# A two-layer graph and expert network on one core: mask casts issued late as transfers, the input in five loads, powers in pairs, and a written-out issue order

## The chip, the cores and the metric

The kernel runs on one core of a Trainium2 chip. The metric is the device time of one execution in microseconds (us). A core has five engines with in-order queues of their own: TensorE (PE, matmuls; PEld, its weight loads), VectorE (DVE), ScalarE (ACT), GpSimd (POOL) and SyncE (SP, which here only issues transfers). Sixteen DMA engines serve the transfers that SyncE, ScalarE and GpSimd issue.

## The reference, cut to what matters

There are 2708 rows of 256 features and a dense 2708 x 2708 matrix `adj` whose non-zero entries are large (up to 1e9, about 1% of all). Each of two layers adds a graph attention and then a block with eight experts to the rows:

```python
# layer 0
x = x + _L0_gnn_ref(_layernorm(x, axis=-1), adj, ...)      # softmax(leaky_relu(..) + adj) @ h
x = x + _L0_ffn_ref((_layernorm(x, axis=-1))[None], ...)   # causal attention, then top-2 of 8 experts
# layer 1
x = x + _L1_gnn_ref(_layernorm(x, axis=-1), adj, ...)      # mask = (adj != 0) | eye; softmax; sigmoid(attn @ Xp)
x = x + _L1_ffn_ref((_layernorm(x, axis=-1))[None], ...)   # top-2 of 8 experts
return x
```

In layer 0 `adj` is added to the logits, so with entries that large each row's softmax picks the row's largest entry: the graph attention is a gather of one projected row. In layer 1 only `adj != 0` matters. The kernel tests on the chip that these readings hold for its input and has a general path behind a flag, which is not run here.

## The kernel before, in words

Rows are worked on in 22 tiles of 128 (the last has 20). There are four stages: `first` (layer 0 up to the router and three early expert blocks), `experts_blocks` of layer 0, `second` (layer 1's graph attention and router), `experts_blocks` of layer 1.

`first` and `second` don't issue their instructions in program order. Each adds steps to a `Plan` (L75): a step has an engine, an assumed length, a function that issues its instructions, the steps that it needs, named buffers that it takes and gives, a rank, and `lands`, the time by which a transfer's data comes after its issue. `issue` (L125) walks an assumed clock: it finds the steps that can start soonest, and among those of one engine that can start within `NEAR` of that it issues the one of lowest rank. That fixes the order in every engine's queue; the chip then runs these queues in order, with waits on semaphores. When TensorE would idle in the plan for `GAP_MIN` or more, `fill` puts filler matmuls (`nobody`, L1288 and L1691: a constant tile against itself) into the gap, `FILL` of it at `UNIT` each.

The first stage, by its steps:

- Loads on SyncE: `x` in three transfers (four tiles, 17 tiles, the last; L856, L859), then weights (L868, L870).
- `project(t0)` for a pair of tiles, eleven in all: `stats` (VectorE mean and variance, L268, L270, L918), `power` (GpSimd, the reciprocal root, one per tile, L922), `turn` (transposes, L929), `bias` (GpSimd, L933), `back` (ScalarE, L938), `times` (matmuls with the centred weight, L949), `out_` (ScalarE scales, L956), `store` (to the DRAM tensor `hd`, issued by ScalarE, L961).
- `tile_in(t)` for a tile: `load` of a row block of `adj` (1354 KB, one of three ring buffers `adj0..2` in `arena`, L990) and of the rope table (L992); `top` (L995) and `index` (L999), VectorE's search for the largest entry and its place; `narrow` (L1009), ScalarE's cast of the block to bf16 in two halves, with GpSimd memsets of the padding (L1006, L1008); `save` (L1012), which stores the halves in the DRAM tensor `mb` for the second stage; `fetch` (L1017), GpSimd's gather of the chosen rows of `hd`, added to the tile; then statistics (VectorE), `power` (GpSimd, L1029, L1030), `norm` and `leave` (ScalarE), transposes and `times` (TensorE, L1038, L1047), the rope in `both` (GpSimd, L804 to L806, L1064) and `turn_qk`, `keep` (L1070, L1073). A ring buffer is taken by `adj` and `low` names: it is free again when both `index` and the second `narrow` have read it. The first `narrow` also waits for the last projected rows in DRAM.
- `pair(t0)`: causal attention of two tiles against all tiles before them. Per earlier tile `scores` (L1121), `exps` (ScalarE, L1127), `mask` on the diagonal (GpSimd, L1136), `values` (L1147), and `sums` (VectorE, L1161, L1166; the first three pairs sum on TensorE). Then `spread`, `turn_over` (VectorE's reciprocal, L1204), `weigh` (GpSimd, L1208), `project_out` (L1222), `join` (L1226), `sum_up` (GpSimd, L1229), `store` (L1232).
- `route` after the pairs at 4, 10, 16, 18 and 20: the router's logits, choice, places, and `send` (L1830), GpSimd's scatters of rows to the experts' lists `xs`.
- At the end three early expert blocks (L562, L585), whose weights go into `arena` when the ring is free, and whose results GpSimd adds to DRAM (L622).

The experts' stage (L2115, L2130) starts with a transfer of rows of `xs` and so after all scatters. `second` reads `mb` with transposing transfers as its masks.

`before` is a constant strict triangle, made by a GpSimd iota and a VectorE comparison (L232); `allones` is set by GpSimd alone (L229).

Of the kernel before, what the change touches and what calls it, by code (L numbers as in the profile page):

```python
# [20 lines left out]
P = 128  # L21
N = 2708
# [51 lines left out]

class Plan:  # L75
# [8 lines left out]
    UNIT = 0.24  # L84
    FILL = 0.75
    GAP_MIN = 1.0
# [38 lines left out]
    def issue(self, behind=0.0):  # L125
# [25 lines left out]
def adj_ffn_kernel(ctx, tc, x, adj, vecs, bias_rows, tab, w_gnn0, w_gnn1, wqkv, wo,  # L151
# [41 lines left out]

    ident = const.tile([P, P], F32, name="ident")
# [33 lines left out]
    allones = const.tile([P, P], F32, name="allones")  # L228
    nc.gpsimd.memset(allones, 1.0)  # L229

# [138 lines left out]

    def route(add, tiles, ready, copied, cleared, layer, XB, xs, pool, turn_tile, turn_bank, gate_tile, gate_bank, rank):  # L370
# [127 lines left out]
        if layer == 0:  # L498
            a = [add("ACT", 0.6, lambda t=t: squares(t), [ready[t - t0]], rank=rank) for t in tiles]
            a = add("DVE", 0.3, mean, a, rank=rank)  # L500
            scaled = add("POOL", 0.9, power, [a], rank=rank)
        last = None
        for pair in pairs:
# [10 lines left out]
            if gate_tile is None:  # L514
                a = add("ACT", 0.25, lambda pair=pair: keep(pair), [a], give=[turn_bank], rank=rank)
            last = a
        a = add("DVE", 3.2, choose, [last], rank=rank)
        b = add("ACT", 0.5, exps, [a], rank=rank)
# [3 lines left out]
        return [add("POOL", 2.7, lambda t=t: send(t), [b, c] + cleared, rank=rank + 6, lands=2.0) for t in tiles]  # L522


    def some_blocks(add, layer, blocks, fetched, needs, weights, xs, acc, new, named, rank):

        joins = []
        for k, (e, j, before) in enumerate(blocks):
# [68 lines left out]
            a = add("ACT", 0.7, back, [a], take=[names["xT"]], give=[names["mm"]], rank=r)  # L597
# [3 lines left out]
            a = add("ACT", 1.4, gate, [a], take=[names["sl"], names["hT"]], rank=r)  # L601
            a = add("DVE", 1.4, times, [a], give=names["up"] + [names["sl"]], rank=r)
# [4 lines left out]
            joins.append(add("POOL", 1.6, join, [a], give=[names["ys"]], rank=r))  # L607
        return joins

    def early_blocks(add, layer, needs, sent, *rest):  # L610
        blocks = [(e, j, (needs if layer == 0 else []) + sum([sent[t] for t in sent if t < before_t], []))
                  for e, j, before_t in EARLY[layer]]
# [196 lines left out]
    def first(X, XB, norms, tops, hd, mb, xs, acc, arena, load_weights):  # L809
# [11 lines left out]
        with ExitStack() as s:  # L821
# [24 lines left out]
            def tr_tile():  # L846
                return mm_tile().rearrange("p (k c) -> p k c", c=P)

            plan = Plan(mm=2, mv=4, ix=4, tb=6, st=2, o=1, zs=1, e=4, xg=3, hT=3,
                        z=2, qk=2, es=1, ob=2, yT=2, mb=2, rT=1, adj0=1, adj1=1, adj2=1, low0=1, low1=1, low2=1)  # L850
# [396 lines left out]
            for t in range(NT):  # L1247
                tile_in(t)
# [1194 lines left out]
```

## Time and profile before

| what | us |
|---|---|
| median of 3 runs | 1467.53 (1466.63 to 1470.84) |
| the profiled execution | 1465.13 |
| its span, first to last instruction | 1463.3 |
| PE busy in the span | 1385.9 (95%) |
| DVE, ACT, POOL busy | 775.9, 555.3, 525.3 |
| mask casts on ACT (L1009), 44 | 57.2, 1323 ns each |
| gathers' issues on POOL (L1017), 22 | 37.2, 1691 ns each |
| filler matmuls of `first` (L1288), 220 | 33.4 |

The profile is of one execution. Busy time is by engine; a matmul's end is modelled, so a busy TensorE isn't one at its peak. "Chain of waits" is the chain of work that ended last, followed back from the last instruction. "Releaser" is what ended an engine's idle time. The granted clock is the share of TensorE's full clock that the throttle let through. Lines like L1009 are lines of the kernel printed above.

### The profile page before, as it was taken

The numbers are of one execution on the slowest core, as the hardware profiler recorded it, in microseconds if no ns is written. First come the engines' busy times: TensorE is split into PE (matmuls) and PEld (weight loads), VectorE is DVE, ScalarE is ACT, GpSimd is POOL, SyncE is SP. The second block draws the span as 40 slices with busy tenths as digits, with TensorE's granted clock in tenths as the row PEclk, the third lists the DMA queues.
The fourth block names the chain that finished last, engine by engine and source line by source line (L and its number), as shares of the span: only waits on it lengthen the run. The fifth ranks groups of instructions, "written<-read, shape, count | busy, mean of one in ns | idle before, by whom it ended". The sixth has DMA issues, their size and how long they took to land.

```text
span 1463.3 us, 20902 instructions
## 1 busy us (share of the span) xinstructions
PE 1385.9 (95%) x7218; PEld 1006.3 (69%) x7218; DVE 775.9 (53%) x1680; ACT 555.3 (38%) x1104; POOL 525.3 (36%) x677
## 2 busy tenths in 40 slices
PE   6988989989999999999999899999999999999996
PEld 5643433433343888888788878888768888878885
DVE  5688999985676432222222474768565322322221
ACT  2576867655545322222221444434432211111110
POOL 5576668874224312222222210022334222222222
PEclk9899999999999999999999999999999999999998
DMA  7588756540001277777512770616321687666211
GB/s 268 192 290 287 252 197 226 158 155 31 8 16 64 46 205 185 168 175 197 105 18 26 159 166 1 133 39 151 108 73 58 148 214 187 194 185 129 24 19 21
DMA packets 260056, 193.05 MB, mean 132 GB/s; under 512 B 168008, under 2 KB 232104, under 8 KB 257232
## 3 DMA queue, kind: packets, MB, share of 16 engines
q1 hardware_dynamic: 235638, 162.32, 38.0%
q0 software_dynamic: 20032, 25.71, 9.7%
q10 hardware_dynamic: 4270, 3.58, 0.8%
q8 instruction: 59, 0.97, 0.3%
q14 instruction: 57, 0.47, 0.1%
HBM read 119.81 MB, written 56.11 MB: 120 GB/s over the span
## 4 chain that ended last, share of the span: by engine, by line
PE 77%; DVE 8%; POOL 6%; DMA 5%; issue 2%; ACT 1%; SPq 0%; POOLq 0%; DVEq 0%; ACTq 0%
PE pup L2115 23%; PE po L1603 15%; PE y L2130 13%; PE o L1147 4%; PE stt L1121 4%; PE up L562 3%; DMA X<-hd,ix 3%; PE pup L2146 3%; PE y L2180 1%; DVE yT L1204 1%; DVE es L1166 1%; PE po L949 1%; DVE ix L999 1%; POOL ra L804 1%; DVE tops L995 1%
## 5 line engine op out<-in xcount | busy, mean ns | idle before, releaser
L2115 PE MATMUL pup<-xTs,arena 128*128 128x256 f32 (+2 forms) x1320 | 249.7, 348 | 0.6 <-ACT xTs L2098 0.6
L2115 PEld LDWEIGHTS pup<-xTs,arena 128*128 128x128 f32 (+1 forms) x1320 | 218.5, 189 | 27.2 <-PE y L2180 1.5
L1603 PE MATMUL po<-hb,PT 128*128 128x257 f32 (+2 forms) x968 | 227.6, 389 | 2.9 <-DVE PT L1596 2.9
L2119 ACT ACTIVATE sl<-pup 128x256 f32<-128x256 f32 (+1 forms) x210 | 73.5, 350 | 368.9 <-PE pup L2115 325.4
L1603 PEld LDWEIGHTS po<-hb,PT 128*128 128x128 f32 (+2 forms) x968 | 176.7, 189 | 42.8 <-issue 13.3
L2120 DVE TENSOR_TENSOR hT<-sl,pup 128x256 f32<-128x256 f32 (+1 forms) x210 | 79.6, 380 | 225.8 <-ACT sl L2119 220.5
L1127 ACT ACTIVATE e<-stt 128x1024 f32<-128x1024 f32 (+1 forms) x132 | 125.5, 986 | 93.5 <-PE stt L1121 63.8
L1166 DVE TENSOR_TENSOR es<-es,e 128x1024 f32<-128x1024 f32 x104 | 137.8, 1325 | 29.8 <-ACT e L1127 22.0
L622 POOL DMA_INDIRECT out<-ys,XR x44 | 68.0, 1545 | 234.2 <-DVE ys L2133 149.5
L622 POOL DMA_INDIRECT acc<-ys,XR x44 | 68.3, 1553 | 215.4 <-DVE ys L2133 120.8
L1121 PE MATMUL stt<-qT,kT 64*128 64x512 f32 (+1 forms) x528 | 133.4, 616 | 4.3 <-ACT e L1127 3.9
L2130 PE MATMUL y<-arena,hT 128*128 128x256 f32 x612 | 137.3, 380 | 0.0
L2130 PEld LDWEIGHTS y<-arena,hT 128*128 128x128 f32 x612 | 114.6, 190 | 19.7 <-DVE hid L2154 4.9
L1830 POOL DMA_INDIRECT xs<-XR,place x88 | 93.2, 1059 | 91.8 <-DVE mk L1590 40.2
L1147 PE MATMUL o<-e,V 128*64 128x512 f32 (+1 forms) x528 | 122.4, 586 | 0.0
L1581 ACT ACTIVATE E<-sb,dcol 128x768 f32<-128x768 f32 (+1 forms) x88 | 75.3, 859 | 108.4 <-DVE PT L1596 106.5
L2133 DVE TENSOR_SCALAR ys<-y,XR 128x256 f32<-128x256 f32 x71 | 34.4, 484 | 133.7 <-PE y L2130 133.7
L2115 PE MATMUL pup<-xTs,room 128*128 128x256 f32 (+3 forms) x528 | 99.9, 346 | 0.0
L1121 PEld LDWEIGHTS stt<-qT,kT 64*128 64x128 f32 x528 | 44.7, 188 | 76.5 <-issue 63.0
L2115 PEld LDWEIGHTS pup<-xTs,room 128*128 128x128 f32 (+1 forms) x528 | 85.4, 189 | 9.8 <-PE y L2180 0.8
L1147 PEld LDWEIGHTS o<-e,V 128*64 128x64 f32 x528 | 32.9, 136 | 68.5 <-issue 53.2
L995 DVE MAX8 tops<-arena 128x8 f32<-128x2708 f32 (+1 forms) x22 | 65.3, 2970 | 1.5 <-DMA arena<-in_adj 1.5
(319 smaller groups left out, 1972.1 us busy)
## 6 DMA issues: line engine op xcount, KB each, us to landing
more<-in_w SPq DMA_DIRECT2D x48, 640.0 KB
arena<-in_adj SPq DMA_DIRECT2D x21, 1354.0 KB
arena<-in_w SPq DMA_DIRECT2D x36, 640.0 KB
mb<-mb SPq DMA_DIRECT2D x44, 352.0 KB
xs<-none SPq DMA_DIRECT2D x16, 536.0 KB
room<-in_w SPq DMA_DIRECT2D x12, 640.0 KB
pieces<-xs SPq DMA_DIRECT2D x200, 32.0 KB
acc<-X SPq DMA_DIRECT2D x21, 128.0 KB
```

What stands on the lines that cost most here:

```text
L622: i = nc.gpsimd.indirect_dma_start(out=acc[:, :], out_offset=bass.IndirectOffsetOnAxis(ap=tokens.bitcast(I32), axis=0), in_=ys, in_offset= ...
L995: nc.vector.max(out=tops[:r, t, :], in_=v["a"][:r])
L1121: nc.tensor.matmul(st[:r, g, c0(sb):], kT[a:b, sb * P:sb * P + r], qT[a:b, t0 + (sb == t0 + 1):t0 + 2, :, :], start=True, stop=True)
L1127: nc.scalar.activation(e[:r, :, c0(sb):], v[sb, "st"][:r, :, c0(sb):], AF.Exp, scale=1.0 / HD ** 0.5)
L1147: nc.tensor.matmul(v["o"][g * HD:(g + 1) * HD, c:], V[:r, sb, g * HD:(g + 1) * HD], v[sb][:r, g, c:], start=(n + i == 0), stop=(n + i == t ...
L1166: nc.vector.tensor_tensor(es, es, v[sb][:r, :, c:], ALU.add)
L1581: nc.scalar.activation(e[:q, :n], sb[:q, i0:i1], AF.Exp, bias=dcol[:q, j:j + 1], scale=SLOPE - 1.0)
L1603: nc.tensor.matmul(v["po", i][:r, :F], v["PT", j][:q, a:a + r], hb[:q, j, :], start=(j == 0), stop=(j == NT - 1))
L1830: i = nc.gpsimd.indirect_dma_start(out=xs[:, :], out_offset=bass.IndirectOffsetOnAxis(ap=at, axis=0), in_=src, in_offset=None)
L2115: nc.tensor.matmul(pp[:to, i, :B, :], wn[:, c, :], xT[:, c, :B, :], start=(c == 0), stop=(c == KC - 1))
L2120: nc.vector.tensor_tensor(hT[:, n, :B, :], sl[:, :B, :], pp[:, 1, :B, :], ALU.mult)
L2130: nc.tensor.matmul(y, hT[:, n, b, :], w[3][:, n, :], start=(n == 0), stop=(n == NHC - 1))
```

## The change

What it does, part by part:

- The mask casts leave `tile_in`. `narrow`, its memsets and `save` go, and the buffers `low0..2` and `mb` with them. In their place stand 22 steps `cast` on GpSimd, each a transfer that reads a row block of `adj` from DRAM a second time and writes it to `mb` as bf16. They need the load of the last tile and, in the plan, one another. A step `blank` on SyncE writes zeros to the padding of `mb`.
- `x` comes in five loads (tiles 0-1, 2-5, 6-13, 14-20, 21). The rope table has a step of its own.
- `project` takes the statistics of two tiles into one buffer and makes one scaling and one `power` for the pair.
- The index results of all tiles have room of their own (`ixs`), not four buffers in turn.
- `allones` is set earlier, and the fillers multiply `allones` by itself. `UNIT` becomes 0.22, `FILL` 0.85, `GAP_MIN` 0.7.
- `issue` takes a list that gives every step its rank: `ORDERS[0]` with 1233 numbers for `first`, `ORDERS[1]` with 1128 for `second`. In the first list the tiles' searches stand as 0, 1, 3, 2, 4, 6, 10, 5, 7, 8, 9, 11, 12, 13, 14, 16, 15, 17, 19, 20, 21, 18; the casts stand between the fourth pair's `weigh` and the last pair's `mask`, the last five gathers among them.
- Assumed lengths and `lands` are changed throughout, and some needs are added that order steps (an expert's `join` after the stores of its rows; one router's choice after the one before; two empty steps at the end of each stage).

```diff
-    UNIT = 0.24
-    FILL = 0.75
-    GAP_MIN = 1.0
+    UNIT = 0.22
+    FILL = 0.85
+    GAP_MIN = 0.7
...
-    def issue(self, behind=0.0):
+    def issue(self, order, behind=0.0):
+        assert len(order) == len(self.steps), len(self.steps)
+        for step, n in zip(self.steps, order):
+            step["rank"] = n
...
-            plan = Plan(mm=2, mv=4, ix=4, tb=6, st=2, o=1, zs=1, e=4, xg=3, hT=3,
-                        z=2, qk=2, es=1, ob=2, yT=2, mb=2, rT=1, adj0=1, adj1=1, adj2=1, low0=1, low1=1, low2=1)
+            plan = Plan(mm=2, mv=4, mvp=4, tb=6, st=2, o=1, zs=1, e=4, xg=3, hT=3,
+                        z=2, qk=2, es=1, ob=2, yT=2, rT=1, adj0=1, adj1=1, adj2=1)
...
-            for a, b in ((0, 4), (4, NT - 1)):
-                loads.append(add("SP", 0.5, lambda a=a, b=b: nc.sync.dma_start(
+            loads, ends = [], (2, 6, 14, NT - 1)
+            for a, b in zip((0,) + ends, ends):
+                loads.append(add("SP", 0.55 * (b - a), lambda a=a, b=b: nc.sync.dma_start(
...
+                def power():
+                    for at, q in [((0, 2), P)] if rows(t0 + 1) == P else [((0, 1), P), ((1, 2), rows(t0 + 1))]:
+                        n = at[1] - at[0]
+                        nc.gpsimd.tensor_tensor(out=rsx[:q, t0 + at[0]:t0 + at[1]], in0=v["pv"][:q, at[0]:at[1], 0],
+                                                in1=mhalf[:q, :n], op=ALU.pow)
...
-                    nc.scalar.copy(m[:r, :b - a], v["a"][:r, a:b])
-
-                def save(h):
-                    nc.sync.dma_start(out=mb[t * P:(t + 1) * P, h * HALF:(h + 1) * HALF], in_=v["m", h])
+                def cast():
+                    nc.gpsimd.dma_start(out=mb[t * P:t * P + r, :N], in_=adj[t * P:t * P + r, :])
...
-                a = loaded[t] = add("SP", 5.8, load, take=[f"adj{t % 3}", f"low{t % 3}", "tb"], rank=rank,
-                                    lands=1.5)
-                a = add("DVE", 2.97, top, [a], rank=rank + 2)
-                b = a
-                for h in range(2):
-
-                    b = add("ACT", 1.4, lambda h=h: narrow(h), [b, stored[-1]], take=["mb"], give=[f"low{t % 3}"] * h, rank=rank + 4)
-                    add("SP", 0.4, lambda h=h: save(h), [b], give=["mb"], rank=rank, lands=3.0)
-                a = add("DVE", 3.05, index, [a], take=["ix"], give=[f"adj{t % 3}"], rank=rank + 2)
+                a = loaded[t] = add("SP", 3.6, load, take=[f"adj{t % 3}"], rank=rank - 2.0, lands=2.0)
+                tb = add("SP", 0.4, load_tb, take=["tb"], rank=rank, lands=2.2)
+                a = add("DVE", 3.0, top, [a], rank=rank)
+                a = add("DVE", 2.97, index, [a], give=[f"adj{t % 3}"], rank=rank)
...
+            add("SP", 3.0, blank, [loaded[NT - 1]], rank=NT + 4.0, lands=3.0)
+            last = None
+            for t, cast in enumerate(casts):
+                last = add("POOL", 1.2, cast, [loaded[NT - 1], last], rank=NT + 0.5 * t, lands=6.0)
...
-                        nc.tensor.matmul(nobody[:, :P], allones, before, start=True, stop=True)
+                        nc.tensor.matmul(nobody[:, :P], allones, allones, start=True, stop=True)
...
-                plan.issue()
+                plan.issue(ORDERS[0])
```

## The prediction

> **What bounds the kernel now.** I read the busy time by stretches first, then the same stretches for the filler matmuls alone, then the chain of waits, then SyncE's queue and the DMA queues. The stretches follow the work: projections (to 60 us), attention limited by VectorE (to 260), attention limited by TensorE (to 480), the tail (to 510), the experts of layer 0 (to 800), the second stage (to 1150), the experts of layer 1. Columns: stretch, length, then busy us of PE, PEld, DVE, ACT and POOL, the granted clock, the DMA share and GB/s.
>
> ```profile
> 0.00:60.00 60.00, 44.37 (x224) 38.17 (x225) 37.48 (x101) 22.01 (x46) 35.12 (x74) 0.89 0.65 213
> 60.00:260.00 200.00, 175.62 (x786) 77.40 (x784) 182.10 (x179) 143.81 (x256) 146.64 (x204) 0.97 0.77 255
> 260.00:480.00 220.00, 209.00 (x958) 82.97 (x957) 160.47 (x205) 121.19 (x192) 107.28 (x135) 1.00 0.21 66
> 480.00:510.00 30.00, 27.55 (x194) 24.71 (x193) 10.79 (x45) 10.12 (x25) 12.79 (x17) 1.00 0.25 51
> 510.00:800.00 290.00, 290.00 (x1622) 245.42 (x1622) 85.83 (x243) 68.55 (x190) 64.09 (x48) 1.00 0.56 136
> 800.00:1150.00 350.00, 339.49 (x1799) 284.51 (x1798) 210.39 (x647) 137.76 (x253) 90.60 (x153) 0.99 0.41 98
> ```
>
> From 510 to 800 us TensorE has no gap, and in the second stage it lacks 10.5 of 350 us. Only the first stage has room. Its fillers are no work, so they come off (the tile `nobody` alone, PE and PEld):
>
> ```profile
> 0.00:60.00 60.00, 11.36 (x60) 10.96 (x61) 0.89 0.65 213
> 60.00:260.00 200.00, 15.38 (x112) 13.97 (x110) 0.97 0.77 255
> ```
>
> TensorE's real work is 44.4 - 11.4 = 33 us of the first 60, 175.6 - 15.4 = 160 of the next 200 (a rate of 0.80), 209.0 - 3.3 = 206 of 220, 27.6 - 3.5 = 24 of 30: 423 us in 510, so 87 us are not work. VectorE is the other bound: 182 of 200 us from 60 to 260, mostly the 44 searches of 2.97 us (L995, L999), which the change keeps. The chain of waits (start, length, what) says what holds both up early:
>
> ```profile
> 9.29 4.10 PE nobody L1288 x22
> 19.44 10.29 DMA hd<-hs
> 57.04 9.35 DMA X<-hd,ix
> 83.15 7.37 DMA X<-hd,ix
> 112.17 10.10 DMA X<-hd,ix
> 166.52 8.48 DMA X<-hd,ix
> 283.30 4.65 DMA X<-hd,ix
> ```
>
> The gather of a tile takes 7.4 to 10.1 us while the DMA engines are 0.77 busy, and 4.65 us when they are quiet. The fillers are the first link on TensorE: they wait for a tile (`before`, L232) that VectorE makes only after four row statistics, and the first transposes (13.2 us) stand behind them although their rows landed at 5.6. In SyncE's queue the reader is to see that nothing is issued between the third mask row load and the first mask save:
>
> ```profile
> 17.92 0.35 SPq L990 DMA_DIRECT2D arena<-in_adj  x1
> ...
> 54.86 1.55 SPq L1012 DMA_DIRECT2D mb<-mb  x2
> 56.51 0.94 SPq L990 DMA_DIRECT2D arena<-in_adj  x1
> ```
>
> The fourth load (56.5 us) is queued behind a save whose ScalarE cast waits for the last projected rows; its buffer was read by the first index search at 38.6.
>
> **The change part by part.** Sums are against the profiled execution: 1465.13 us, of which 1463.3 are the span; it lies 2.4 us under the median of the three runs (1467.53).
>
> *Fillers from `allones` on both sides.* That tile is set by GpSimd at 2.4 us. The fillers can run from there, and the first real transposes start when two row tiles (256 KB instead of 512 KB) have landed, 4 to 6 us instead of 13.2. Gain at the head between 0 (if the projections are then held by the store of 10.29 us or by VectorE's 22 statistics, 22 x 0.76 = 17 us) and 9. More filler (0.85 of a gap from 0.7 us on) costs at most one filler run before a real step, some 1 us each for a few dozen runs, from 0 to 10 in all. I take 8 off for the head and 0 for the runs, since they are sized to gaps.
>
> *X in five loads.* The same 2.7 MB; four more issues on SyncE by 0.48 us, beside the landing of the first. Nothing.
>
> *Powers in pairs.* 11 of 22 powers of 0.55 us go (6 us of POOL) and 10 scalings of 0.15 on VectorE. Off the chain; each pair's first power now waits for the second tile's statistics, 0.76 us, hidden behind the matmuls of 1.9. Nothing.
>
> *The casts leave ScalarE.* 44 casts of 1.32 us = 57 us go from ScalarE before 295 us, 47 of them before 240, and with them 44 saves (15.5 MB) from SyncE and the DMA engines, and 10.7 us of memsets from POOL. SyncE no longer blocks at 18 to 55 us, and a mask row buffer comes free at the index search. What is late next is VectorE itself: it was idle 60 - 37.5 = 22.5 us before 60 and 17.9 from there to 260, some 40 us, of which about 6 at the start can't be filled. 40 of the saves, 14 MB of some 64 moved (213 GB/s for 60 us, 255 for 200), fall before 260, so the DMA share drops by about a fifth. Four gathers on the chain at 4.65 instead of 35.3 in all is 16.7 us at best, 0 at worst (the loads may run ahead and fill the engines again).
>
> *The casts come back as 22 transfers from DRAM to DRAM, issued by POOL.* The issue: no row shows one. Nearest are the gathers' issues, 1.46 to 2.44 us, median 1.64: 22 x 1.64 = 36 us of POOL. The list puts the first one behind the fourth pair's weighting (L1208, 184 us in this trace) and the last one before the masks of the last pair, so nearly all lies in a stretch where POOL has 220 - 107 = 113 us free. Behind each on POOL are masks, scatters and the rope of late tiles; a delay of 1.6 us there is covered by e's four buffers. Without that cover it would be the 36 us.
>
> The Trainium skill, "SBUF — State Buffer", in its warning on DVE blocking DMA, speaks against this: descriptors of a DMA issued by GpSimd can't be written while VectorE holds the shared port, and 620 ns became 3100. By that the casts would take 22 x 3.1 = 68 us of POOL, an estimate that still fits into those 113; the gathers' issues here rose to 2.44 at most beside a VectorE 91% busy.
>
> Their transfers: POOL's queue q0 took 9.7% of 16 engines' span for 25.71 MB, which is 88 engine-us per MB; SyncE's q1 took 38.0% for 162.32 MB, 55. A tile of 1.39 MB read is thus 4.8 us (q1's rate) to 7.7 (q0's), and 11.5 if the 0.69 MB written count too. I take 7.7, q0's, since it is the same queue: 22 x 7.7 = 169 us beside a DMA share of 0.21. It costs nothing on the path if it is over when the last scatters need the same queue (near 480 us).
>
> The DRAM padding (seven issues, some 3 us of SyncE) and two empty steps at each stage's end stand where SyncE idles. The added needs (a row's store before an expert's join, one router's choice after the last) order steps in the plan; the same DRAM rows and tiles order them on the chip now. Nothing.
>
> *The order.* The first list takes tiles as 0, 1, 3, 2, 4, 6, 10, 5 and leaves the search of tile 18 until behind the sixth pair's reciprocal; in this trace all searches are over at 294 us, before the seventh. So 6 to 12 us of VectorE can move out of the stretch where it is the bound into one where it is 73% busy. No row shows an order that was not run: from 10 us lost (a wait in the wrong place on an in-order engine) to 15 gained. I keep 4 of it.
>
> *The sum.* Head 8. In the stretch of 160 us of real work I expect a rate of 0.89 instead of 0.80: VectorE's idle 18 us nearly filled, and late searches moved out. 160 / 0.89 = 180, 20 us less (about 10 by gathers, 6 by buffers and ScalarE, 4 by order). After 260 us there are 230 us of work in 250; I take 2. Together 30: 1465 - 30 = **1435 us**. The second stage's list, read against the order that the kernel issues now, moves 6 of SyncE's 40 steps and 5 of POOL's 73, none by more than 3 places: 0, with -3 to +3.
>
> **The rivals.** *More than that:* the rate reaches 0.97, a little above the 0.94 (206 of 220) of the stretch behind it. 160 / 0.97 = 165, 35 off, head 12, tail 8: 55 off, 1410. For it: 87 us aren't work. Against: VectorE's searches, sums and reciprocals are unchanged.
>
> *VectorE stays the bound:* it is 91% busy from 60 to 260, and the moved casts weren't its work. Then the head's 8 and little more: 1450 to 1460. If the new order also adds waits of as much: 1465, no change.
>
> *Slower: the scatters stand behind the casts.* Both go through q0. Started near 200 us, 22 casts end at 480 if each takes 12.7 us; from there on every further us costs 22. At 15 us each they end at 530, the last scatters land behind that, and the experts, which read all scattered rows first, start near 535 instead of 509.5: 25 us later, 1490. For it: q0 moves bytes at under two thirds of q1's rate, and 11.5 us is within the bounds. Against: 12.7 isn't.
>
> *The change does not do what it says:* the casts might be issued early, beside the loads. The list rules it out for most, since each needs the last listed tile's load.
>
> **How the numbers follow.** Forecast (1420 to 1450) 0.52; more 0.13; VectorE's bound with a small gain 0.15; no change 0.06; slower 0.14. Faster by over 0.3% (4.4 us, about what a measurement of this kernel can tell): 0.80; within: 0.06; slower: 0.14. The range reaches from 1405 to 1468, which leaves out the slow case and a little of the fastest.
>
> **What would show it.** Right: real transposes before 8 us; mask loads without the gap from 18 to 55; gathers of 4 to 6 us on the chain; ACT's casts gone; the first matmul of the experts (509.5) at about 480; casts of 5 to 9 us each, over by 430; the second stage as long as before. Wrong: TensorE waiting near 480 for rows whose scatters are late, or VectorE's busy share from 60 on unchanged with the sixth reciprocal still near 257 us.

## The result, and the profile after

The changed kernel takes 1463.79 us (median of 20 runs, 1458.77 to 1468.37), the kernel before, run beside it, 1466.43 (20 runs). The ratio is 0.9986, with a 95% interval of 0.9976 to 0.9995: some 2 us, where 30 were forecast. The profiled execution took 1458.77 us, the fastest of the 20. Its span is 1456.3 us, 7.0 below the profiled span of before.

The stretches of the changed kernel, in the columns of the prediction (PE, PEld, DVE, ACT, POOL, clock, DMA share, GB/s):

```profile
0.00:60.00 60.00, 48.45 (x247) 40.24 (x248) 38.99 (x96) 19.32 (x43) 29.53 (x62) 0.89 0.75 244
60.00:260.00 200.00, 178.29 (x791) 77.97 (x791) 186.89 (x184) 105.20 (x232) 159.08 (x199) 0.97 0.68 199
260.00:480.00 220.00, 216.09 (x1002) 87.99 (x999) 155.03 (x202) 114.37 (x184) 108.30 (x144) 1.00 0.48 110
480.00:510.00 30.00, 29.29 (x209) 27.43 (x208) 12.64 (x57) 8.53 (x19) 10.86 (x19) 1.00 0.42 100
800.00:1150.00 350.00, 342.51 (x1824) 288.23 (x1824) 217.98 (x684) 139.52 (x258) 87.80 (x154) 0.99 0.42 104
```

The fillers of the second of these stretches alone (the tile `nobody`, PE and PEld):

```profile
60.00:260.00 200.00, 15.67 (x114) 14.32 (x112) 0.97 0.68 199
```

ScalarE lost its casts (555 us busy before, 503 now) and the DMA share from 60 to 260 fell from 0.77 to 0.68, an eighth where a fifth was forecast. VectorE's 182 us there became 187. Without fillers TensorE's work from 60 to 260 is 162.6 us, a rate of 0.81 where 0.80 was before and 0.89 was forecast. From 260 to 480 it is 214.6 against 205.8.

The chain of waits (start, length, what) has five gathers again, in sum not shorter (42.4 us, before 40.0), a clear of the experts' lists (`xs<-none`) that was not on it before, and at its end fillers:

```profile
75.36 8.98 DMA X<-hd,ixs
114.99 9.16 DMA X<-hd,ixs
141.55 9.13 DMA X<-hd,ixs
162.56 7.59 DMA X<-hd,ixs
189.75 10.73 DMA xs<-none
283.39 7.57 DMA X<-hd,ixs
494.77 6.70 PE nobody L1404 x60
```

To see where time goes I follow five events through each trace: the issue of the first gather on GpSimd, three of VectorE's eleven reciprocals (`turn_over`, one per pair), and the first matmul (`pup`) of the experts of layer 0. The sixth reciprocal, before and after:

```profile
256.70 3.34 DVE L1204 RECIPROCAL yT<-pm 128x512 f32<-128x512 f32 x1
```

```profile
257.86 3.34 DVE L1303 RECIPROCAL yT<-pm 128x512 f32<-128x512 f32 x1
```

All kernels by these events (us from the span's start), and their ratio to the kernel before on the same chip; 0.001 is 1.5 us:

| kernel | first gather | 6th recip. | 7th | last | experts | ratio (95%) |
|---|---|---|---|---|---|---|
| before | 53.0 | 256.7 | 294.2 | 476.7 | 508.4 | |
| after | 56.2 | 257.9 | 291.8 | 467.5 | 502.7 | 0.9986 (0.9976 to 0.9995) |
| after_again | 54.9 | 255.8 | 289.8 | 468.7 | 503.9 | 0.9975 (0.9958 to 0.9993) |
| head_only | 48.6 | 253.3 | 294.8 | 479.8 | 511.2 | 1.0001 (0.9987 to 1.0015) |
| ob4 | 47.1 | 250.2 | 284.9 | 462.1 | 497.3 | 0.9933 (0.9913 to 0.9953) |
| shift_late | 55.3 | 261.2 | 294.6 | 470.3 | 505.4 | 1.0009 (0.9996 to 1.0022) |
| casts_only | 57.1 | 269.8 | 309.7 | 491.0 | 522.8 | 1.0108 (1.0091 to 1.0125) |
| casts_lands | 57.0 | 254.4 | 292.2 | 486.2 | 518.0 | 1.0053 (1.0037 to 1.0068) |
| casts_early | 59.5 | 257.4 | 294.9 | 480.5 | 512.3 | 1.0002 (0.9992 to 1.0013) |
| casts_early_ob4 | 48.4 | 248.6 | 285.0 | 470.2 | 502.0 | 0.9959 (0.9944 to 0.9974) |
| no_list | 49.3 | 255.9 | 293.8 | 477.1 | 512.3 | 1.0063 (1.0040 to 1.0086) |
| ob4_own1 | 46.5 | 249.4 | 287.3 | 470.6 | 505.7 | 0.9976 (0.9964 to 0.9988) |
| late_search | 50.5 | 253.6 | 305.0 | 481.9 | 517.0 | 1.0019 (1.0001 to 1.0038) |
| half_before | 51.5 | 242.3 | 281.7 | 464.6 | 496.3 | 0.9946 (0.9926 to 0.9966) |
| half_after | 55.6 | 243.4 | 278.1 | 453.8 | 488.9 | 0.9876 (0.9851 to 0.9902) |
| no_end | 55.5 | 256.6 | 290.4 | 466.2 | 500.7 | 1.0031 (1.0015 to 1.0047) |
| no_end_again | 55.3 | 259.3 | 293.8 | 471.1 | 505.4 | 0.9997 (0.9985 to 1.0010) |
| ob4_no_end | 46.3 | 251.2 | 284.4 | 461.4 | 495.8 | 0.9928 (0.9901 to 0.9956) |
| own2 | 55.1 | 257.4 | 291.4 | 468.7 | 503.9 | 0.9962 (0.9949 to 0.9976) |
| ob4_own2 | 46.3 | 250.0 | 283.9 | 461.2 | 496.4 | 0.9903 (0.9881 to 0.9925) |

The two rows of the changed kernel (after, after_again) differ by 0.0011, 1.6 us, with overlapping intervals; a difference to it below is uncertain by as much.

The first two rows, and their traces, give the ledger of the change. Up to the first gather 3.2 us are lost. From there to the sixth reciprocal 2.0 are gained, from the sixth to the last 10.4. From the last reciprocal to the experts 3.5 are lost (31.7 became 35.1). That makes 5.8 at the experts. Up to the second stage's first matmul 0.4 are lost, in that stage 3.7 gained, for a part by the clock's dips (below), and in the experts of layer 1 another 2.0 lost: 7.0 in all, within rounding. That is the difference of two single executions; the medians differ by 2.6 us.

### The profile page after: what moved, and what is told of

Its sections match the earlier page's. It is cut to its first block, busy times and chain, and to the rows that moved or that the text cites. A ratio compares the mean times of both kernels' runs of the same rounds, so it can differ in the third digit from the quotient of the medians.

```text
span 1456.3 us, 20830 instructions
## 1 busy us (share of the span) xinstructions
PE 1394.8 (96%) x7292; PEld 1012.4 (70%) x7292; DVE 776.6 (53%) x1670; ACT 503.1 (35%) x1060; POOL 528.6 (36%) x666
## 4 chain that ended last, share of the span: by engine, by line
PE 74%; DVE 8%; POOL 7%; DMA 4%; issue 2%; ACT 1%; SPq 0%; POOLq 0%; DVEq 0%; ACTq 0%
PE pup L2241 23%; PE po L1719 15%; PE y L2256 13%; PE stt L1220 3%; DMA X<-hd,ixs 3%; PE up L662 3%; PE o L1246 3%; PE pup L2272 3%; DVE ixs L1111 2%; POOL xs L1956 2%; DVE tops L1108 2%; PE y L2306 2%; DVE es L1265 1%; PE pn L1618 1%; PE pt L685 1%
## 5 line engine op out<-in xcount | busy, mean ns | idle before, releaser
L1719 PE MATMUL po<-hb,PT 128*128 128x257 f32 (+2 forms) x968 | 224.5, 386 | 1.2 <-DVE PT L1712 1.2
L1719 PEld LDWEIGHTS po<-hb,PT 128*128 128x128 f32 (+2 forms) x968 | 174.7, 187 | 39.6 <-issue 12.3
L1226 ACT ACTIVATE e<-stt 128x1024 f32<-128x1024 f32 (+1 forms) x132 | 126.1, 987 | 81.0 <-PE stt L1220 55.1
L1265 DVE TENSOR_TENSOR es<-es,e 128x1024 f32<-128x1024 f32 x104 | 133.9, 1287 | 24.3 <-ACT e L1226 18.5
L1956 POOL DMA_INDIRECT xs<-XR,place x88 | 98.0, 1113 | 114.1 <-DVE mk L1706 45.1
L2259 DVE TENSOR_SCALAR ys<-y,XR 128x256 f32<-128x256 f32 x71 | 34.4, 484 | 131.8 <-PE y L2256 131.8
L1111 DVE FIND_INDEX8 ixs<-tops,arena 128x8 uint32<-128x2708 f32 (+1 forms) x22 | 65.4, 2972 | 0.0
```

Source lines behind the costliest of these rows:

```text
L1111: nc.vector.max_index(out=ixs[:r, t, :], in_max=tops[:r, t, :], in_values=v["a"][:r])
L1226: nc.scalar.activation(e[:r, :, c0(sb):], v[sb, "st"][:r, :, c0(sb):], AF.Exp, scale=1.0 / HD ** 0.5)
L1265: nc.vector.tensor_tensor(es, es, v[sb][:r, :, c:], ALU.add)
L1719: nc.tensor.matmul(v["po", i][:r, :F], v["PT", j][:q, a:a + r], hb[:q, j, :], start=(j == 0), stop=(j == NT - 1))
L1956: i = nc.gpsimd.indirect_dma_start(out=xs[:, :], out_offset=bass.IndirectOffsetOnAxis(ap=at, axis=0), in_=src, in_offset=None)
```

## The experiments

Theory 1 was that VectorE bounds the stretch up to the sixth reciprocal, so that work taken from ScalarE and the DMA engines is worth nothing. Theory 2 was that parts of the change gain what they should and other parts give it back. Theory 3 was that only the listed order gains.

### The head

head_only: the kernel before with early fillers and the input in five loads, the sum for the centred weight being allowed ahead of these loads (an excerpt of the edit):

```diff
-            for a, b in ((0, 4), (4, NT - 1)):
+            loads, ends = [], (2, 6, 14, NT - 1)
+            for a, b in zip((0,) + ends, ends):
...
-            wg_in = add("SP", 0.0, lambda: None, rank=-9.0, lands=3.0)
+            wg_in = add("SP", 0.0, lambda: None, rank=-9.5, lands=3.0)
...
-                        nc.tensor.matmul(nobody[:, :P], allones, before, start=True, stop=True)
+                        nc.tensor.matmul(nobody[:, :P], allones, allones, start=True, stop=True)
```

> The kernel before with the head's part alone: fillers from the tile of ones on both sides, X in five loads, and the sum for centring the projection weights allowed ahead of the X loads, which the planner needs to find an order. Theory 1 (VectorE is bound from 60 us on): real transposes start before 9 us, but the time moves by no more than the first searches do: first gather 0 to 4 us earlier than 53.0, time 1462 to 1467. Forecast's step (head worth 8): first gather at 45, time 1458. Rival for the head (stores of projected rows wait behind loads, two buffers): transposes early, projections end at 46 to 50 as before, time within 2 us of before.

The first gather comes 4.4 us earlier, the sixth reciprocal 3.4, the seventh is late by 0.6 and the time is the same. The gain of the head is spent before 295 us: VectorE's wait for gathers from 60 to 260 rose from 13.8 to 18.6 us.

ob4: the changed kernel with four buffers for projected rows. The attention outputs of the pairs (`osb`) use the same buffers later and get four as well (two of the four places edited):

```diff
-                        z=2, qk=2, es=1, ob=2, yT=2, rT=1, adj0=1, adj1=1, adj2=1)
+                        z=2, qk=2, es=1, ob=4, yT=2, rT=1, adj0=1, adj1=1, adj2=1)
...
-                    v["hs"] = ab.tile([P, 2 * W2], F32, tag="osb", name="hs").rearrange("p (t c) -> p t c", t=2)
+                    v["hs"] = ab.tile([P, 2 * W2], F32, tag="osb", name="hs", bufs=4).rearrange("p (t c) -> p t c", t=2)
```

> The changed kernel with four buffers instead of two for projected rows (hs, osb) in the plan and on the chip. If the head's gain was lost because ScalarE waits for stores of hd (15 us of waits before 45): projections end at 44 to 47 instead of 51.7, the first gather is issued at 48 to 51 instead of 56.2, and by theory 1 (VectorE takes over from there) the time falls by no more than 4 us, 1459 to 1463. Rival (the stores themselves are slow beside the loads, so the gather waits for the last of them anyway): first gather at 55 to 57, time as now.

This is where the head went. ScalarE writes projected rows to one of two buffers and must wait until the store of the one before last has landed. The timeline of ScalarE in the changed kernel (start, length, line, what, and in brackets its idle time and releaser):

```profile
23.87 0.84 ACT L1065 ACTIVATE hs<-po,rsx 128x256 f32<-128x256 f32 x2 [6.15 <-DMA hd<-hs]
25.63 0.84 ACT L1065 ACTIVATE hs<-po,rsx 128x256 f32<-128x256 f32 x2
32.65 0.84 ACT L1065 ACTIVATE hs<-po,rsx 128x256 f32<-128x256 f32 x2 [3.48 <-DMA hd<-hs]
33.99 0.84 ACT L1065 ACTIVATE hs<-po,rsx 128x256 f32<-128x256 f32 x2 [0.50 <-DMA hd<-hs]
40.93 0.84 ACT L1065 ACTIVATE hs<-po,rsx 128x256 f32<-128x256 f32 x2 [5.63 <-DMA hd<-hs]
```

From 0 to 60 us these waits come to 17.0 us in five places; before it was one of 6.0. The buffers alone don't make them that long: no_list (below), with the same two buffers but the first stage issued without the list, has three of 6.9 in all and issues its first gather at 49.3. ScalarE's waits (for what, us, times, longest), in the changed kernel and in no_list:

```profile
ACT hs L1065 <- DMA hd<-hs: 17.0, 5, 6.1
ACT hs L1065 <- DMA hd<-hs: 6.9, 3, 2.8
```

So the list's order of transfers belongs to the cause. A fuller set of DMA engines doesn't explain it: they are 0.87 busy in the first 40 us, 0.75 before, but 0.93 in no_list. With four buffers no such wait is left, the last projected rows are scaled at 40.4 instead of 52.1, and the first gather is issued 9.1 us earlier than in the changed kernel. The lead is 7.7 us at the sixth reciprocal, 5.4 at the experts, and 0.0053 of the ratio, 7.8 us, in the time (6.2 against after_again); I had expected no more than 4. The lead shrinks on the way, so the attention's own two further buffers add nothing that shows.

shift_late: VectorE's longest wait in the head, 12.3 us for a one-column sum that stands behind the last projections on TensorE, is taken out of its queue.

```diff
-        a = add("PE", 0.3, sum_up, [a], take=["mm"], rank=rank)
-        add("DVE", 0.2, shifted, [a], give=["mm"], rank=rank)
+        postponed.extend([sum_up, shifted])
+        a = add("PE", 0.3, lambda: None, [a], take=["mm"], rank=rank)
+        add("DVE", 0.2, lambda: None, [a], give=["mm"], rank=rank)
...
                     nc.vector.reciprocal(v["yT"].rearrange("p t j c -> p (t j c)"), v["z"])
+                    while postponed:
+                        postponed.pop(0)()
```

> The changed kernel with the one-column sum and the shift that VectorE waits 12.3 us for moved behind the first reciprocal; the rest of the order as it is. Theory 1: one or two searches fit into that wait, the sixth reciprocal comes 3 to 8 us earlier than 257.9, time 1456 to 1461. Rival (the head is held by the stores of projected rows, and VectorE waits there for something else instead): sixth reciprocal within 2 us, time 1462 to 1466.

One search moves up, then VectorE waits 8.7 us for the next sum behind the same projections; the sixth reciprocal is 3.3 us later, the experts 2.7, and the time 0.0023 worse, outside both expectations. The longest wait of an engine was not the one that held the work. (Part of the time is the granted clock in the second stage, told below.)

### Late casts under the order of before

casts_only leaves everything but the casts as before (`narrow` and `save` go, `cast` and `blank` come); three more kernels change one thing more each.

```diff
+                    nc.gpsimd.dma_start(out=mb[t * P:t * P + r, :N], in_=adj[t * P:t * P + r, :])
...
+                last = add("POOL", 1.2, cast, [loaded[NT - 1], last], rank=NT + 0.5 * t, lands=6.0)
```

> The kernel before with one part of the change: the casts leave ScalarE and come back as 22 late transfers; planner, order rules, fillers and X loads as before. Theory 1 (VectorE is the bound up to the sixth reciprocal, and the casts were not its work): sixth reciprocal within 4 us of 256.7, time within 5 us of before (1466), though ScalarE's busy time from 60 to 260 falls by some 40 us. Theory 2 (the part gains what was forecast for it, some 16 us by gathers and buffers, and another part of the change gave it back): sixth reciprocal at 238 to 245, time 1448 to 1454. Theory 3 (only the listed order gains, the rest is nothing): as theory 1.

Neither theory foresaw it: 16 us slower. The plan puts VectorE's statistics of a tile (L268) 2.5 us behind its gather; the gathers on the chain take 4 to 11, and the searches that could run meanwhile stand behind the statistics in VectorE's queue. Its waits from 60 to 260 us (for what, us, times, longest):

```profile
DVE st L268 <- DMA X<-hd,ix: 26.1, 8, 9.2
```

casts_lands changes one number of casts_only.

```diff
-                a = add("POOL", 1.6, fetch, [a, biased[t]] + stored, give=["ix"], rank=rank, lands=2.5)
+                a = add("POOL", 1.6, fetch, [a, biased[t]] + stored, give=["ix"], rank=rank, lands=6.5)
```

> The kernel before with late casts (as in casts_only), and the landing of a gather planned at 6.5 us instead of 2.5. Theory A (late casts alone lost 16 us because the planner, rid of the casts, put VectorE's statistics too early behind gathers that take 7 to 9 us: it waited 26.1 us for them instead of 13.8): VectorE's wait for gathers from 60 to 260 below 12 us, sixth reciprocal at 255 to 262 instead of 269.8, time 1466 to 1474. Rival (late casts cost by themselves, by their transfers or by POOL): wait smaller, but sixth reciprocal still near 268, time 1480 or more.

With the landing planned at 6.5 us the wait falls to 4.3 and the sixth reciprocal is 15 us earlier, as the expectation's theory A said:

```profile
DVE st L268 <- DMA X<-hd,ix: 4.3, 1, 4.3
```

Half the loss stays, behind the seventh reciprocal. The last casts are issued up to 470 us, and the chain of casts_lands shows a fetch of scattered rows beside them, one of three issued together for the early expert blocks. TensorE waits 4.18 us for the first of the three (below) and 0.91 for the next:

```profile
467.92 2.85 DMA xs<-XR,place
471.33 9.51 DMA XR<-xs
```

```profile
479.28 0.69 PE L540 MATMUL pm<-ident,XR 128*128 128x128 f32 x2 [4.18 <-DMA XR<-xs]
```

In the same kernel a fetch at 514.8 us, when the casts are over, takes 2.21 us; in casts_only, with casts up to 480, the early blocks' fetch takes 5.5.

casts_early changes one line of casts_lands.

```diff
-                last = add("POOL", 1.2, cast, [loaded[NT - 1], last], rank=NT + 0.5 * t, lands=6.0)
+                last = add("POOL", 1.2, cast, [loaded[16], last], rank=16.0 + 0.5 * t, lands=6.0)
```

> casts_lands with the casts allowed from the seventeenth mask row's load on instead of from the last one's, so that they run some 50 us earlier and are over before the last scatters. If their place beside the last scatters and fetches is the rest of the loss: no fetch of scattered rows above 5 us on the chain behind 460 us, last reciprocal at 474 to 480 instead of 486.2, time 1464 to 1469, ratio 0.998 to 1.002. Rival (the casts cost wherever they stand): last reciprocal within 3 us of 486, ratio 1.004 or more.

Issued from 201 to 400 us the casts are out of the way: TensorE takes up the same rows 4.1 us after their fetches are first issued (at 472.2), without a wait for them (below). The last reciprocal comes 5.7 us earlier (still 3.8 behind before), and the time is that of before. Late casts, with the landing planned at 6.5 us, are worth nothing under the old order, neither gain nor loss. The kernel before with only that landing changed was not run, so what each of the two is worth isn't known.

```profile
476.30 0.66 PE L540 MATMUL pm<-ident,XR 128*128 128x128 f32 x4
```

casts_early_ob4 adds ob4's edit.

> casts_early with four buffers for projected rows, which fit only where the casts' tiles are gone. If the buffers bring the head forward whatever the order: first gather 4 to 9 us earlier than in casts_early, ratio 0.004 to 0.006 below it. Rival (they help only behind the change's early fillers and small X loads): first gather within 2 us, ratio within 0.002.

The first gather comes 11 us earlier and the ratio falls by 0.0043. So the buffers pay without the list and without early fillers. With four buffers the change's own head adds little: its first gather is at 46.5 to 47.1 us (ob4_own1, ob4) where the old head has 48.4 here.

### The order

no_list and ob4_own1 issue the first stage by the ranks given in the code, with the change's other parts.

```diff
-                plan.issue(ORDERS[0])
+                plan.issue([s["rank"] for s in plan.steps])
```

> The changed kernel with the first stage issued by the ranks that its steps are given, not by the list. Theory 1: sixth reciprocal at 254 to 262, time 1460 to 1470; what differs lies behind the seventh reciprocal. Theory 2 (the list gave back what the casts gained): faster than the changed kernel by 5 to 15 us, 1449 to 1459, sixth reciprocal before 250. Theory 3 (the list is what gains): slower than the changed kernel by 6 to 12 us, 1470 to 1476, and the lead of 9 us behind the seventh reciprocal gone.

> ob4 with the first stage issued by its steps' own ranks, not by the list. If the list's gain lies behind the seventh reciprocal and is its own: seventh to last reciprocal 181 to 185 us instead of ob4's 177, time 6 to 12 us above ob4, ratio 0.998 to 1.002. If the buffers bring it whatever the order: ratio within 0.002 of 0.9933.

The list is worth 0.0077 of the ratio without and 0.0043 with four buffers, 11 and 6 us. In the traces it is where theory 3 put it: from the seventh to the last reciprocal 183.3 us in both kernels without the list, 182.5 in the kernel before, but 175.7 in the changed one and 177.2 in ob4. From the sixth to the seventh it gains 3 to 4 more (33.9 and 34.7 against 37.9 in both). At the head it loses: the first gather of no_list is 6.9 us earlier than the changed kernel's. no_list even led by 12 us at the fourth reciprocal (172.9 against 185.4) and had lost it at the fifth; why was not looked into.

late_search is ob4 with the searches of the last two tiles held behind the sixth reciprocal too, as I had read the list to do with tile 18.

```diff
+            for t, end in ((20, 751), (21, 751)):
+                for n in (1, 2, 3):
+                    plan.steps[123 + 16 * t + n]["needs"].append(plan.steps[end])
```

> ob4 with the searches of the last two tiles, and their rotation tables' loads, held until behind the sixth reciprocal: 38 searches ahead of it instead of 42, 12 us of VectorE out of the stretch where it is the bound. The forecast's step on the order (late searches moved out of that stretch gain 6 to 12): sixth reciprocal 6 to 12 us earlier than ob4's 250.2 and the lead kept to the end, 1450 to 1456. Rival (TensorE is the bound behind it, and the late tiles' projections and scores then come too late there): sixth reciprocal earlier by 4 to 10, but the last reciprocal 0 to 15 us later than ob4's 462.1, time 1461 to 1476.

The sixth reciprocal comes 3.4 us later than in ob4, the seventh 20, the time is 12.6 us worse. Both expectations missed the first half: with four searches fewer to do VectorE is not faster, it waits (3.9 us in ob4):

```profile
DVE st L364 <- DMA X<-hd,ixs: 15.7, 6, 7.4
```

Searches of late tiles are what VectorE does while a gather is under way. The held steps also moved the head's order: the first gather is 3.4 us late, as late as the sixth reciprocal. From one to the other it takes 203.1 us in ob4 and 203.2 here, so four searches less shorten that stretch by nothing.

### VectorE's share

half_before and half_after search only half of the columns (`index` is cut in the same way).

```diff
-                    nc.vector.max(out=tops[:r, t, :], in_=v["a"][:r])
+                    nc.vector.max(out=tops[:r, t, :], in_=v["a"][:r, :N // 2])
```

> The kernel before with each search over the first 1354 of 2708 columns only, so that the neighbours it finds are those of half the graph; 44 searches of some 1.5 us instead of 2.97, 65 us of VectorE less, nothing else moved. Theory 1 (VectorE bounds up to the sixth reciprocal): sixth reciprocal at 215 to 235 instead of 256.7, time 15 to 35 us below before, 1432 to 1451. Rival (gathers, mask loads or TensorE bound that stretch): sixth reciprocal later than 248, time within 8 us of before.

> The changed kernel with the same halved searches. Theory 1, if VectorE also hides what the freed ScalarE and transfers are worth: it gains more than the kernel before does from the same cut, so that it ends 10 to 25 us below half_before. Rival (the freed work is worth nothing wherever VectorE stands): within 5 us of half_before, as the uncut pair is.

VectorE falls from 187 to 151 us busy in the 200 (here half_after), and TensorE rises only from 178 to 187:

```profile
60.00:260.00 200.00, 186.82 (x840) 81.02 (x839) 150.63 (x196) 112.19 (x243) 171.12 (x208) 0.99 0.73 210
```

The sixth reciprocal comes 14.4 us earlier in both, for some 60 us of searches less before it, which lies between the two expectations of half_before. So VectorE is a part of that bound, a quarter by this count, and not the whole of it. Without fillers TensorE's rate rises to 0.86 in half_after.

What takes over can be read from the traces. VectorE waits for gathers instead; its waits from 60 to 260 us in the kernel before, in half_before, in the changed kernel and in half_after:

```profile
DVE st L268 <- DMA X<-hd,ix: 13.8, 6, 4.1
DVE st L268 <- DMA X<-hd,ix: 32.5, 11, 6.0
DVE st L364 <- DMA X<-hd,ixs: 5.2, 5, 1.6
DVE st L364 <- DMA X<-hd,ixs: 23.8, 11, 6.0
```

And the chain of waits passes to other engines. Summed by engine from its rows between the first gather and the sixth reciprocal, some 202 us in the changed kernel are 84 of VectorE, 46 of transfers, 36 of GpSimd and 21 of TensorE; some 188 in half_after are 53 of GpSimd, 52 of TensorE, 37 of transfers, 22 of SyncE's queue and 10 of VectorE. From 200 to 250 us GpSimd, with scatters, rope and casts, is 93% busy in both (before, 88%; its spans are rough in a profile); the changed kernel (POOL, clock, DMA share, GB/s):

```profile
200.00:250.00 50.00, 46.60 (x58) 0.99 0.59 153
```

No run here was made to lighten GpSimd in that stretch, so what that would bring is open.

The changed kernel does gain more time from the cut (0.0110 against 0.0054), as theory 1 allowed. But in the traces its experts start 13.7 us earlier and those of the kernel before 12.2, so most of that difference arises behind them and is not explained.

### The tail and the second stage

no_end, no_end_again (the same kernel) and ob4_no_end put the empty closing step on SyncE, so that no fillers stand in front of the experts.

```diff
-            add("PE", 0.5, lambda: None, [a], rank=999.0)
+            add("SP", 0.5, lambda: None, [a], rank=999.0)
```

> The changed kernel with the empty closing step on TensorE put on SyncE: 30 fillers (60 matmuls as counted, 6.7 us) in front of the experts go, nothing else. Theory 2's tail (the fillers stand in front of rows that have landed): the experts' first matmul 33.5 to 34.5 us behind the last reciprocal's start instead of 36.3, time 2 us below the changed kernel, some 1461.5. Rival (the rows land only when the fillers end, or the clock falls without them): 36 us as now, time 1463 to 1465.

> no_end once more. If its fillers are worth what no_end showed: ratio 1.001 to 1.004, and dips of the clock in the second stage that after_again does not have. If they cost in the tail (0.7 us) what they save in clock: ratio within 0.0015 of after_again's.

> ob4 without the fillers that the empty closing step puts in front of the experts: the second look at what no_end showed. Theory (they hold the granted clock through the wait for the last scattered rows, and a dip there is followed by others): granted clock below 0.92 from 490 to 510, mean clock 0.003 to 0.005 below ob4's, time 4 to 8 us above ob4, a ratio of 0.996 to 0.999. Rival (no_end's 1473 was the spread of runs): ratio within 0.001 of 0.9933.

The timeline of TensorE in no_end, and its stretch from 490 to 510 us (columns here: PE, clock, DMA share, GB/s):

```profile
493.28 0.28 PE L2353 MATMUL y<-hsum,allones 128*128 128x8 f32 x2
498.44 0.69 PE L2219 MATMUL pt<-ident,XR 128*128 128x128 f32 x2 [4.87 <-DMA XR<-xs]
```

```profile
490.00:510.00 20.00, 14.29 (x63) 0.83 0.64 165
```

TensorE waits 4.87 us, the granted clock falls to 0.83 over those 20 us (1.00 in the changed kernel), and the matmuls behind run slower: from the last reciprocal to the experts it is 34.5 us instead of 35.1, and the experts up to the second stage's first matmul take 301.0 instead of 299.4. no_end_again and ob4_no_end repeat it: waits of 5.17 and 5.30 us, a clock of 0.83, 34.3 and 34.4 us, 301.3 and 301.1. So in the traces the fillers cost 0.6 us and save 1.6. In the times the three kernels disagree: without fillers 6.6 us slower, 3.2 slower, 0.7 faster (differences of ratios to the same kernel with them; the last two with overlapping intervals). What they are worth stays open between these. Nor does a dip there bring more of them in the second stage: by the count told below no_end loses 6.8 us to dips there, where the changed kernel loses 3.4, but no_end_again 1.7, and ob4_no_end 5.1 where ob4 loses 6.8.

The Trainium skill, "TensorE: Matmul & The Clock Gate", section "HAM oscillation — how this bites in real kernels", gives as its rule no idle gaps of TensorE above some 3.4 us, since its clock is throttled after them. These three gaps agree with it; no run here shows where the limit lies. It doesn't explain all of the dips inside the second stage, told below.

own2 and ob4_own2 issue the second stage by its own ranks (`plan.issue(ORDERS[1])` replaced as above); after_again is the changed kernel once more.

> The changed kernel itself, for a second profile and times on the chip of the next three. If the profile's short second stage (336.7 us from its first matmul to the experts of layer 1, where other kernels with the same list show 342 to 346) was luck of the clock: 339 to 346 here; the first stage the same within 1.5 us (experts' first matmul at 501 to 504); ratio to before 0.997 to 1.000.

> The changed kernel with the second stage issued by its steps' own ranks. If the second list costs 2 to 4 us: ratio 0.995 to 0.997, second stage 333 to 338 us. If it is worth nothing: the ratio of after_again, 339 to 346 us.

> The changed kernel with four buffers for projected rows (ob4) and the second stage issued by its steps' own ranks instead of the list. If the second list costs what the traces hint (337 to 346 us from its first matmul to the experts of layer 1 in five traces with it, 340 to 344 in four without): 1 to 4 us below ob4, a ratio to before of 0.991 to 0.993. If the list is worth nothing either way: within 0.1% of ob4's 0.9933. If the list gains there: 0.995 or more.

after_again's second stage, from its first matmul to that of layer 1's experts, takes 336.5 us, as in the first profile (336.7); it was not luck of one run. own2's takes 336.8, ob4_own2's 334.8: in the traces the list gains nothing. Yet the listed stage takes 342.8 in no_end, 344.2 in ob4 and 346.0 in shift_late. The granted clock by slices of 10 us tells a part of it, half in the first two and nearly all in the third: the time lost to dips there (10 us less the clock's share, summed) is 3.4 us in the changed kernel, in own2 and in ob4_own2, 6.8, 6.8 and 12.0 in those three, and 5.1 before. In several of these slices TensorE is busy throughout by the profile's count, as in this one of the changed kernel (PE, clock, DMA share, GB/s):

```profile
1040.00:1050.00 10.00, 10.00 (x36) 0.83 0.91 316
```

In time, own ranks are 0.0013 (own2) and 0.0030 (ob4_own2) better, with overlapping intervals. ob4_own2 is the fastest kernel here that searches all columns: 1453.27 us, 0.9903 of before.

## Why the prediction was wrong, by its steps

**Head, 8 us: mis-sized by its own condition.** The transposes start at 7.6 us, as listed. The text said the gain would be 0 "if the projections are then held by the store", and then took 8. They were: 17.0 us of waits for stores, 3.2 us lost at the first gather, and the list's order made these waits longer (6.9 without it). ob4's 7.8 us look like the forecast's 8, but that is luck: they are the price of two more buffers, of which casts_early_ob4 has 6.3 with the old head. head_only, the head's part alone, gains 4.4 us at the first gather and nothing in the time.

**Gathers, 10 us: failed.** The DMA share fell, the gathers did not: 7.6 to 9.2 us on the chain where 4.65 was taken. In the 20 us slices in which the first four start the share is 0.68, 0.84, 0.93 and 0.51, so even beside half-idle engines a gather took 7.6. Loads and clears run ahead, as the forecast's "0 at worst" allowed (14 mask loads and 8 clears from 60 to 180 us, before 12 and 6); that they slow the gathers was not tested. And the price was taken from the wrong view: VectorE waited 13.8 us for gathers in that stretch, not 35.3. That wait did fall, to 5.2, and VectorE filled it with searches for later tiles.

**Buffers and ScalarE, 6 us: failed.** casts_early, with the casts off ScalarE and a mask row buffer free at the index search, stands at 1.0002.

**The rate of 0.89 from 60 to 260: the step that failed.** 0.81 was measured, and from the first gather to the sixth reciprocal 2.0 us were gained where 20 were forecast. The step took idle time of VectorE, once filled, for TensorE's work moved up. VectorE's idle time fell only from 17.9 to 13.1 us, and what filled it belongs to tiles that no pair needs yet: the sixth pair needs 12 tiles, and 21 are searched before its reciprocal. That reciprocal stands at 257.9, which was the forecast's own sign against it. half_before and half_after show that even 60 us less VectorE bring it only 14 forward; gathers, GpSimd and TensorE then share the chain. What would shorten that stretch most stays open.

**X in five loads, powers in pairs, nothing:** head_only agrees for the first; the powers were not tried alone.

**Order, 4 us: right in sign, wrong in mechanism.** The list's numbers are ranks; the planner issues whatever can start. Tile 18's two searches do stand behind the sixth reciprocal, but in the kernel before four did: 42 of 44 are ahead of it now, 40 before. They moved into the stretch, not out. The gain is behind it.

**After 260 us, 2 us: mis-sized, 10.4 from the sixth to the last reciprocal.** There TensorE's rate rose from 0.94 to 0.98, with the list. Which of its placements does that I did not separate.

**Empty closing steps, nothing: mis-sized.** The tail is 3.5 us longer. Fillers of 6.7 us stand in front of the experts, but without them only 0.6 to 0.8 of it comes back.

**Casts: right in size, and cheaper to issue.** The issues and landings in the changed kernel (ns least, median, most; then us):

```profile
L1115 POOL DMA_DIRECT2D mb<-in_adj x22: 520/576/1244, 190.0 to 387.0; - x22
...
DMA to landing us min/median/max: 6.1/8.0/15.1
```

8.0 us each where 7.7 was taken, the last issued at 387 (over by 430 was forecast), and 0.58 us of POOL each where 1.64 was. Three of the casts were issued beside a VectorE 93% busy (190 to 260 us), the others beside one 74% busy, and the slowest issue took 1.24 us. The 3.1 us worked out from the Trainium skill's warning on DVE blocking DMA in "SBUF — State Buffer" were not seen. That warning is about VectorE operations in a two-port mode; whether any of those here ran in one the trace doesn't show.

**The rivals.** The time fits "no change" best, which had 0.06; "VectorE stays the bound", at 0.15, named the right sign, but would have kept the head's 8. "Scatters behind casts" did not come about in the changed kernel. casts_lands shows something like it in small where the casts run up to 470 us: there a fetch right behind a scatter is late.

## What to carry to other kernels

A gain at the head of a pipeline passes through every buffer count on the way: price it with the wait that is next, here a store out of one of two buffers, before it enters a sum. Idle time of a busy in-order engine isn't room for the critical work unless what it would do there is what the next stage lacks; count whose tiles it would serve. When one engine's work is cut and the end moves by a quarter of it, look at who waits next before cutting more. When a step leaves, the order that a planner finds changes everywhere, so an assumed latency (2.5 us for a gather that takes 4 to 11) may cost more than the step was worth: 8 us here.

## What the runs showed of the hardware

A GpSimd transfer that casts 1.39 MB from DRAM to DRAM cost 0.58 us to issue and 8.0 to land. In casts_lands a fetch of scattered rows took 9.5 us beside such transfers and another 2.2 without. Three gaps of TensorE of 4.9 to 5.3 us each came with a granted clock of 0.83 over 20 us, where kernels without the gap had 1.00. The second stage by one list took 336 to 346 us, with 1.7 to 12 us lost in dips of the granted clock; what sets them off where TensorE has no gap was not found.
